# Layer norms brought to features on partitions by 32 by 32 turns on VectorE and two transfers, in place of turns by TensorE

## The chip, the cores and the metric

The kernel runs on one core of a Trainium2 chip. The time is the device time of one launch in microseconds (us). TensorE (PE in the profile) multiplies, VectorE (DVE), ScalarE (ACT) and GpSimd (POOL) do the rest, and SyncE (SP) issues every DMA of this kernel[...].

## What is computed

Four transformer blocks in sequence on x of 16 batches x 256 tokens x 256 features, in float32, 16 heads of 16 features, with a context of 77 tokens per batch and one condition vector per batch. Cut to what matters:

```python
# each of the ten steps below begins with a layer norm of x over the features
def step_norm(x):                         # statistics per token
    h = (x - mean(x)) * rsqrt(var(x) + eps)
    return h * (1 + scale[b]) + shift[b]  # per batch and feature; one step has no modulation

# block 0: self attention with rope and mask (a), attention to the context (ac), MLP (b)
# block 1: attention to the context (cx)
# block 2: self attention (c), attention to the context (cc), MLP (d)
# block 3: self attention with rope (e), attention to the context (ec), MLP (f)
x = x + gate * (softmax(q @ k.T) @ v) @ wo          # attention steps
x = x + gate * (gelu(step_norm(x) @ w1 + b1) @ w2)  # MLP steps, 1024 hidden
```

## The kernel before

x stays in SBUF as x_sb, with tokens on partitions: 128 partitions x (16 batches, 2 halves, 256 features). A matmul contracts over partitions, so a projection of the normed x needs it with features on partitions. `norm_tasks` makes that, once per batch and step, 160 times in all: VectorE takes mean and variance (L467, L468), GpSimd the power -1/2 and the scaled difference xn (L473, L474, L495), TensorE turns xn by four 128x128 transposes through the identity into one PSUM bank (L503), and ScalarE takes the bank into xT with the modulation as scale and bias (L510, or L507 in step cc, which has none). xT is read by the projections (L592 without rope, L644 with rope, L764 for v) or by the first MLP matmul (L1015).

The rest of an attention: scores per head group (L805 self, L817 context), row maxima on VectorE (L831, L835, L839), and these maxima go through DRAM to stand as an extra row beside the queries (L851 turn, L854 store to mrow, L858 load into the tile kq). Then the scores again, transposed and with the maxima in them (L902), exp on ScalarE (L914, L916), the product with v (L925), turns and division (L934, L941, L947, L951), and the output projection with the residual (L972, L978, L985, L988). MLP hidden activations are L1020, the second matmul is L972 too. Gates are loaded by L540 (gb tiles), and L528 adds a bias early.

Nothing is in program order by hand. Every step is a task with an engine, an estimated duration, dependencies and the buffers that it takes or uses (`add`), and a planner (`Order.solve`) runs these through a list schedule. It fixes the order of each engine's instructions, SP's queue among them, before the kernel is built. TensorE takes the ready task with the lowest `prio`, which rises from batch to batch and from step to step; VectorE, ScalarE and GpSimd take what has been ready longest. A transfer has the cost `ISSUE` on SP, 0.45 us, and then a latency `lat`, plus 2.7 us per MB where the task gives a size. [...]

Buffers are counted in `CAPS`: 8 PSUM banks (`b`), one xn, two xT, five kq. A batch is admitted to an attention when a kq tile is free, and holds it until its last L902. The MLP steps wait for all norms of the attention step ahead (`join(norms)`) and, for their matmuls, for its last exponentials. `BY_PE = 2` marks the first two batches of step a, whose mask is added by TensorE.

Of the kernel before, what the change touches and what calls it, by code (L numbers as in the profile page):

```python
# [10 lines left out]
F32 = mybir.dt.float32  # L11
U8 = mybir.dt.uint8
AF = mybir.ActivationFunctionType
# [3 lines left out]
B, N, D, H, HD, LC, FF = 16, 256, 256, 16, 16, 77, 1024  # L17
P = 128
NT = N // P
NC = D // P  # L20
# [53 lines left out]
class Order:  # L74
# [12 lines left out]
    def add(self, eng, dur, run, deps=(), take=(), use=(), prio=0, rp=None, kind=None, joins=(),  # L87
            line=None, last=True, more=0.0, lat=0.0, first=False, mb=0.0):


        t = Task()
        t.joins, t.line, t.last, t.more, t.lat, t.first, t.mb = joins, line, last, more, lat, first, mb
        t.eng, t.dur, t.run, t.prio, t.rp, t.kind = eng, dur, run, prio, rp, kind
        t.deps = [d for d in deps if d is not None]
        t.take, t.held = list(take), list(take) + list(use)
        for h in t.held:
            h.users += 1
        t.outs, t.left, t.ready, t.no, t.since = [], len(t.deps), 0.0, len(self.tasks), None
        for d in t.deps:
            d.outs.append(t)  # L100
        self.tasks.append(t)
        return t
# [111 lines left out]
def pixart_kernel(ctx: ExitStack, tc: tile.TileContext, x, cond_t, ctx_in, mask_c, mask_s, tables, vecs, rows,  # L214
                  mod0, mod1, mod2, mod3, wa, wb, wc, wd, we, wf, out):
    nc = tc.nc
# [4 lines left out]

    CAPS = {"b": 8, "xn": 1, "xT": 2, "kq": 5, "v": 5, "mx": 3, "mr": 2, "ec": 2,
            "ts": 2, "oT": 2, "rope": 2, "qk": 4, "tmp": 2, "gb": 3, "wa": 1, "ctx": 2,
            "cin": 2, "bias": 2, "small": 4, "csmall": 2}

    const = ctx.enter_context(tc.tile_pool(name="const", bufs=1))
    wpool = ctx.enter_context(tc.tile_pool(name="weights", bufs=1))
    work = ctx.enter_context(tc.tile_pool(name="work", bufs=2))
    small = ctx.enter_context(tc.tile_pool(name="small", bufs=4))
    dram = ctx.enter_context(tc.tile_pool(name="dram", bufs=1, space=bass.MemoryType.DRAM))  # L230
# [46 lines left out]
    mrs, vs = [], []  # L277
    for j in range(CAPS["mr"]):
        mrs.append(dram.tile([2, 2, 4, 512], F32, name=f"mrow{j}"))

    for j in range(CAPS["v"]):
        vs.append(const.tile([P, NT, H, 32], F32, name=f"vt{j}"))
# [2 lines left out]
    add = od.add  # L285
    MM = 0.432
    TR = 0.109
    ISSUE = 0.45
    BY_PE = 2
# [40 lines left out]
    t = add("PE", 0.4, rows_turn, take=[h_rt], prio=200)  # L330
    add("DVE", 1.3, late_consts, deps=[t], use=[h_rt], prio=200)
    late_t = od.tasks[-1]
    t = add("ACT", 0.3, silu_exp, prio=200)
# [37 lines left out]
    mods, mod_t = {}, {}  # L371
# [107 lines left out]
    def join(tasks, prio=0):  # L479
        return add("NO", 0.0, lambda: None, deps=tasks, prio=prio)  # L480

    def norm_tasks(s, b, eps, mod, name, prio, deps=()):

        hs, hn, hm, ht = Hold("small"), Hold("xn"), Hold("b"), Hold("xT")

        def stats():
            s["mv"] = norm_stats(x_sb[:, b], P, NT, name)

        def rstd():
            s["rstd"] = rstd_of(s["mv"], P, NT, eps, name)  # L490

        def scale():
            xn = s["xn"] = work.tile([P, NT, D], F32, tag="xn", bufs=CAPS["xn"], name=f"xn_{name}")
            for t in range(NT):
                nc.gpsimd.tensor_scalar(xn[:, t, :], x_sb[:, b, t, :], s["mv"][:, t, 0:1], s["rstd"][:, t:t + 1],  # L495
                                        ALU.subtract, ALU.mult)

        def turn():
            pt = s["pt"] = psum(hm, NC)
            s["xT"] = work.tile([P, NC, N], F32, tag="xT", name=f"xT_{name}")  # L500
            for c in range(NC):
                for t in range(NT):
                    nc.tensor.transpose(pt[:, c, t * P:(t + 1) * P], s["xn"][:, t, c * P:(c + 1) * P], ident)  # L503

        def take():
            if mod is None:
                nc.scalar.copy(s["xT"], s["pt"])  # L507
            else:
                for c in range(NC):
                    nc.scalar.activation(s["xT"][:, c, :], s["pt"][:, c, :], AF.Identity,  # L510
                                         scale=mods[mod][:, 2 + c, b:b + 1], bias=mods[mod][:, c, b:b + 1])
        t1 = add("DVE", 1.0, stats, deps=[x_done[b], *deps], take=[hs], prio=prio)
        t2 = add("POOL", 0.95, rstd, deps=[t1], use=[hs], prio=prio)
        t3 = add("POOL", 2.5, scale, deps=[t2], take=[hn], use=[hs], prio=prio)
        t4 = add("PE", 4 * TR, turn, deps=[t3], take=[hm, ht], use=[hn], prio=prio)
        t5 = add("ACT", 0.6 if mod is None else 1.1, take, deps=[t4, mod_t.get(mod)], use=[hm, ht], prio=prio)
        x_done[b] = t3
        return t5, ht

    def early_add(s, b, pre_add, prio):  # L520

# [164 lines left out]
        a = add("PE", NC * nt * TR, turn, deps=deps, take=[hm], use=[h_dst, *hq], prio=prio)  # L686
        return take(lambda: u["p"], a, [hm, h_dst], prio)

    state = {"mr": 0}

    def attention(b, name, n, wv, wkeys, h_w, w_t, eps, mod, half, biases, masked, pre_add, gate, prio, ctxs=None,
                  barrier=None, after=None, norm_deps=()):

        s, nm = {}, f"{name}{b}"
        self_ = n == N
# [9 lines left out]
        def admit():  # L705
# [5 lines left out]
                  take=[h_kq, h_v], prio=prio,  # L711
                  joins=[("mx", nm), ("mr", nm)] +
                        [(i, (nm, g, kc)) for i in ("e", "av") for g in range(NC) for kc in range(nk)])
        admitted.append(x_t)
        xT_t, hx = norm_tasks(s, b, eps, mod, nm, prio, deps=[x_t])

        norms.append(xT_t)
        if self_:
# [6 lines left out]
        if half is None:  # L725
            hm1, hm2, u = Hold("b"), Hold("b"), {}
# [126 lines left out]
        def move_out():  # L853
            nc.sync.dma_start(s["mr"][0].rearrange("s r (c i j) -> i (s r c) j", i=4, j=32), s["mt"])  # L854

        def move_in():
            for i in range(2):
                nc.sync.dma_start(s["kq"][HD * i:P:32, i], s["mr"][:, i].rearrange("k r n -> r k n"))  # L858
# [491 lines left out]
```

## Time and profile before

| what | value |
|---|---|
| time, median of 3 runs | 2684.58 us (2683.35 to 2687.24) |
| the profiled execution: its time, its span | 2684.49 us, 2682.7 us |
| TensorE busy | 2635.8 us, 98% of the span |
| VectorE, ScalarE, GpSimd busy | 1542.2, 1240.1, 1065.7 us |
| moved by DMA | 60.25 MB |
| granted clock of TensorE, mean | 0.995 |

How to read it: a busy time is the union of the records of an engine; TensorE's matmuls are pipelined, so that the mean duration of one record says less than the distance from group to group. A float32 matmul has two records, a turn one. In a timeline row stand the start, the duration, the engine, the line, the operation, the tile written and the tiles read, the shapes and the count; in brackets stand the engine's idle time ahead of it and what ended it. PEld is the loading of weights into the array.

### The profile page before, as it was taken

The numbers are of one execution on the slowest core, as the hardware profiler recorded it, in microseconds if no ns is written. First come the engines' busy times: TensorE is split into PE (matmuls) and PEld (weight loads), VectorE is DVE, ScalarE is ACT, GpSimd is POOL, SyncE is SP. The second block draws the span as 40 slices with busy tenths as digits, with TensorE's granted clock in tenths as the row PEclk, the third lists the DMA queues.
The fourth block names the chain that finished last, engine by engine and source line by source line (L and its number), as shares of the span: only waits on it lengthen the run. The fifth ranks groups of instructions, "written<-read, shape, count | busy, mean of one in ns | idle before, by whom it ended". The sixth has DMA issues, their size and how long they took to land.

```text
span 2682.7 us, 56475 instructions
## 1 busy us (share of the span) xinstructions
PE 2635.8 (98%) x22144; PEld 1887.2 (70%) x22144; DVE 1542.2 (57%) x4379; ACT 1240.1 (46%) x2495; POOL 1065.7 (40%) x1413
## 2 busy tenths in 40 slices
PE   8999999999999999999999999999999999999999
PEld 5656665766888667666666667888666666667888
DVE  7788886664320566766775664111788876883100
ACT  2444444664332456455555554232455555553332
POOL 4333332545443445133334544433333333562321
PEclk9999999999999999999999999999999999999999
DMA  4000000012110000100000012000000000000000
GB/s 145 14 7 9 10 7 14 16 52 90 31 39 12 25 17 6 35 13 13 20 16 9 5 33 66 16 20 16 11 4 4 4 3 6 5 21 24 20 20 20
DMA packets 53570, 60.25 MB, mean 22 GB/s; under 512 B 19592, under 2 KB 38264, under 8 KB 52536
## 3 DMA queue, kind: packets, MB, share of 16 engines
q1 hardware_dynamic: 53304, 56.65, 7.1%
q8 instruction: 174, 2.85, 0.4%
q14 instruction: 92, 0.75, 0.1%
HBM read 50.44 MB, written 6.19 MB: 21 GB/s over the span
## 4 chain that ended last, share of the span: by engine, by line
PE 92%; DVE 3%; POOL 2%; ACT 1%; issue 1%; DMA 1%; DVEq 0%; ACTq 0%; POOLq 0%; SPq 0%
PE bank L972 20%; PE bank L902 13%; PE bank L1015 12%; PE bank L925 11%; PE bank L805 7%; PE bank L592 7%; PE bank L644 6%; PE bank L764 5%; PE bank L503 3%; PE bank L817 2%; PE bank L684 2%; PE bank L895 2%; PE bank L388 1%; PE bank L579 0%; ACT e_ac L914 0%
## 5 line engine op out<-in xcount | busy, mean ns | idle before, releaser
L902 PE MATMUL bank<-kq 32*128 32x256 f32 (+1 forms) x5120 | 606.2, 396 | 2.9 <-DMA kq<-mrow 2.5
L902 PEld LDWEIGHTS bank<-kq 32*128 32x128 f32 (+1 forms) x5120 | 354.3, 168 | 158.4 <-issue 108.2
L805 PE MATMUL bank<-kq 32*128 32x512 f32 x1536 | 411.1, 638 | 1.9 <-DVE kq L617 1.8
L831 DVE CUSTOM_DVE_ANT_0 junk<-bank,ctxT_masks 128x256 f32<-128x256 f32 x448 | 188.7, 421 | 52.5 <-PE bank L805 21.4
L916 ACT ACTIVATE e_a<-bank 128x512 f32<-128x512 f32 x256 | 137.8, 597 | 175.0 <-PE bank L805 147.1
L916 ACT ACTIVATE e_e<-bank 128x512 f32<-128x512 f32 x256 | 136.1, 599 | 143.9 <-PE bank L805 105.2
L835 DVE TENSOR_REDUCE mx_c<-bank 128x2 f32<-128x512 f32 x256 | 160.2, 681 | 36.8 <-PE bank L805 36.2
L916 ACT ACTIVATE e_c<-bank 128x512 f32<-128x512 f32 x256 | 134.9, 601 | 100.3 <-PE bank L805 74.8
L835 DVE TENSOR_REDUCE mx_e<-bank 128x2 f32<-128x512 f32 x256 | 161.1, 681 | 26.5 <-PE bank L805 25.4
L978 DVE TENSOR_TENSOR x_sb<-x_sb,bank 128x512 f32<-128x512 f32 x80 | 54.8, 685 | 202.3 <-PE bank L972 193.4
L817 PE MATMUL bank<-kq 32*128 32x154 f32 x2048 | 166.9, 309 | 1.3 <-DVE mx_ec L839 0.5
L805 PEld LDWEIGHTS bank<-kq 32*128 32x128 f32 x1536 | 127.4, 184 | 25.2 <-issue 8.1
L817 PEld LDWEIGHTS bank<-kq 32*128 32x128 f32 x2048 | 130.0, 185 | 17.2 <-issue 6.8
L1020 ACT ACTIVATE h_d<-bank,vec 128x256 f32<-128x256 f32 x128 | 53.7, 471 | 156.0 <-PE bank L1015 105.8
L1020 ACT ACTIVATE h_f<-bank,vec 128x256 f32<-128x256 f32 x128 | 53.6, 471 | 153.4 <-PE bank L1015 132.2
L1020 ACT ACTIVATE h_b<-bank,vec 128x256 f32<-128x256 f32 x128 | 53.6, 471 | 146.2 <-PE bank L1015 118.6
L1015 PE MATMUL bank<-xT_b,kq 128*128 128x256 f32 x512 | 113.8, 379 | 0.0
L1015 PE MATMUL bank<-xT_d,kq 128*128 128x256 f32 x512 | 113.6, 380 | 0.0
L1015 PE MATMUL bank<-xT_f,kq 128*128 128x256 f32 x512 | 113.4, 379 | 0.0
L972 PE MATMUL bank<-kq,h_b 128*128 128x256 f32 x512 | 113.2, 379 | 0.0
L972 PE MATMUL bank<-kq,h_d 128*128 128x256 f32 x512 | 113.2, 379 | 0.0
L972 PE MATMUL bank<-kq,h_f 128*128 128x256 f32 x512 | 113.2, 379 | 0.0
(336 smaller groups left out, 5751.4 us busy)
## 6 DMA issues: line engine op xcount, KB each, us to landing
kq<-in_mod_dram SPq DMA_DIRECT2D x10, 512.0 KB
cin<-in_ctx_in_dram SPq DMA_DIRECT2D x36, 128.0 KB
x_sb<-in_x_dram SPq DMA_DIRECT2D x16, 256.0 KB
gb_b<-gate_g0m SPq DMA_DIRECT2D x16, 256.0 KB
gb_c<-gate_g2a SPq DMA_DIRECT2D x16, 256.0 KB
gb_d<-gate_g2m SPq DMA_DIRECT2D x16, 256.0 KB
out_dram<-x_sb SPq DMA_DIRECT2D x16, 256.0 KB
kq<-mrow SPq DMA_DIRECT2D x224, 16.0 KB
```

Source lines behind the costliest of these rows:

```text
L592: nc.tensor.matmul(dst[:, g, :], lhsT=w[:, k, g * P:(g + 1) * P], rhs=xT[:, k, :], start=(k == 0), stop=(k == NC - 1))
L644: nc.tensor.matmul(u["p"][0:r, at:at + D], lhsT=xT()[:, k, t * P:t * P + r], rhs=w()[:, k, :], start=(k == 0), stop=(k == NC - 1))
L805: ls.append(lambda ps=ps, R=R, keys=keys: nc.tensor.matmul(ps.rearrange("p (s k) -> p s k", k=N), lhsT=s["qx"][R, 0, g, t * P:(t + 1) * P] ...
L817: ls.append(lambda ps=ps, R=R, keys=keys, tt=tt: nc.tensor.matmul(ps[:, 2 * tt * n:2 * (tt + 1) * n].rearrange("p (s k) -> p s k", k=n), l ...
L831: nc.vector.tensor_tensor_reduce(junk, u[i][:, i2 * N:(i2 + 1) * N], mb[:, t, :], -1.0, 3.0e38, ALU.add, ALU.min, m[:, i2, g, t:t + 1])
L835: nc.vector.tensor_reduce(m[:, :, g, t], u[i].rearrange("p (s k) -> p s k", k=N), AX.X, ALU.max, negate=True)
L902: (lambda ps=u[i], R=R, q=q: nc.tensor.matmul(ps[0:rows_n, q * N:(q + 1) * N], lhsT=s["kz"][R, q, g, kc * P:kc * P + rows_n], rhs=s["qx"][ ...
L916: nc.scalar.activation(e, u[i][0:rows_n], AF.Exp)
L925: nc.tensor.matmul(u5["p"][32 * r:32 * r + 32, 1 - q, :], lhsT=s["v"][0:rows_n, kc, 8 * g + 2 * r + 1 - q, :], rhs=s["e", g, kc, r][0:rows ...
L972: nc.tensor.matmul(u["p"][:, t, :], lhsT=lhsT(k, t), rhs=w()[:, k, :], start=(k == 0), stop=(k == nk - 1))
L1015: nc.tensor.matmul(u["p"][:, j, :], lhsT=wv["w1"][:, k, f * P:(f + 1) * P], rhs=s["xT"][:, k, :], start=(k == 0), stop=(k == NC - 1))
L1020: nc.scalar.activation(s["h", i][:, j, :], u["p"][:, j, :], func, bias=vcol(b1, 2 * i + j))
```

## The change

Of the 160 norms, 158 no longer go through TensorE; the two of step a with batches 0 and 1 (`direct`) keep the turn by the array. For the others xn is turned by one VectorE instruction in 32 by 32 blocks into y (`turn32`), which reads features with a stride of four, so that later runs are 512 bytes long. y is stored to DRAM (`move_out`, 128 rows of 2 KB), and loaded again with features on partitions into xr (`move_in`, 512 runs of 512 bytes). ScalarE takes xr into xT with the modulation (`take_in`, two instructions). y and xr have one buffer each, the DRAM rows yd two. No PSUM bank is held by these norms. The planner gets the new tasks with their estimates and makes a new order for all engines.

```diff
--- before.py
+++ after.py
@@ -221,7 +221,7 @@
 
     CAPS = {"b": 8, "xn": 1, "xT": 2, "kq": 5, "v": 5, "mx": 3, "mr": 2, "ec": 2,
             "ts": 2, "oT": 2, "rope": 2, "qk": 4, "tmp": 2, "gb": 3, "wa": 1, "ctx": 2,
-            "cin": 2, "bias": 2, "small": 4, "csmall": 2}
+            "y": 1, "yd": 2, "xr": 1, "cin": 2, "bias": 2, "small": 4, "csmall": 2}
 
     const = ctx.enter_context(tc.tile_pool(name="const", bufs=1))
     wpool = ctx.enter_context(tc.tile_pool(name="weights", bufs=1))
@@ -277,6 +277,8 @@
     mrs, vs = [], []
     for j in range(CAPS["mr"]):
         mrs.append(dram.tile([2, 2, 4, 512], F32, name=f"mrow{j}"))
+
+    yds = [dram.tile([P, 512], F32, name=f"yd{j}") for j in range(CAPS["yd"])]
 
     for j in range(CAPS["v"]):
         vs.append(const.tile([P, NT, H, 32], F32, name=f"vt{j}"))
@@ -479,7 +481,7 @@
     def join(tasks, prio=0):
         return add("NO", 0.0, lambda: None, deps=tasks, prio=prio)
 
-    def norm_tasks(s, b, eps, mod, name, prio, deps=()):
+    def norm_tasks(s, b, eps, mod, name, prio, deps=(), direct=False):
 
         hs, hn, hm, ht = Hold("small"), Hold("xn"), Hold("b"), Hold("xT")
 
@@ -512,10 +514,43 @@
         t1 = add("DVE", 1.0, stats, deps=[x_done[b], *deps], take=[hs], prio=prio)
         t2 = add("POOL", 0.95, rstd, deps=[t1], use=[hs], prio=prio)
         t3 = add("POOL", 2.5, scale, deps=[t2], take=[hn], use=[hs], prio=prio)
-        t4 = add("PE", 4 * TR, turn, deps=[t3], take=[hm, ht], use=[hn], prio=prio)
-        t5 = add("ACT", 0.6 if mod is None else 1.1, take, deps=[t4, mod_t.get(mod)], use=[hm, ht], prio=prio)
         x_done[b] = t3
-        return t5, ht
+        if direct:
+            t4 = add("PE", 4 * TR, turn, deps=[t3], take=[hm, ht], use=[hn], prio=prio)
+            return add("ACT", 0.6 if mod is None else 1.1, take, deps=[t4, mod_t.get(mod)], use=[hm, ht], prio=prio), ht
+
+        hy, hd = Hold("y"), Hold("yd")
+
+        def turn32():
+            s["y"] = work.tile([P, 4, NT * NC * 32], F32, tag="y", bufs=CAPS["y"], name=f"y_{name}")
+            nc.vector.transpose(s["y"].rearrange("p f (u i) -> p f u i", i=32),
+                                s["xn"].rearrange("p t (c j f) -> p f (t c) j", j=32, f=4))
+
+        def move_out():
+            s["yd"] = yds[state["yd"] % len(yds)]
+            state["yd"] += 1
+            nc.sync.dma_start(s["yd"], s["y"].rearrange("p f n -> p (f n)"))
+
+        def move_in():
+            s["xr"] = work.tile([P, 4, NT, NC, 32], F32, tag="xr", bufs=CAPS["xr"], name=f"xr_{name}")
+            nc.sync.dma_start(s["xr"].rearrange("p a t c i -> p a (t c i)"),
+                              s["yd"].rearrange("(a j) (f n) -> (j f) a n", j=32, f=4))
+
+        def take_in():
+            s["xT"] = work.tile([P, NC, N], F32, tag="xT", bufs=CAPS["xT"], name=f"xT_{name}")
+            for c in range(NC):
+                to = s["xT"][:, c, :].rearrange("p (t a i) -> p t a i", t=NT, a=4)
+                of = s["xr"][:, :, :, c, :].rearrange("p a t i -> p t a i")
+                if mod is None:
+                    nc.scalar.copy(to, of)
+                else:
+                    nc.scalar.activation(to, of, AF.Identity, scale=mods[mod][:, 2 + c, b:b + 1],
+                                         bias=mods[mod][:, c, b:b + 1])
+        hr = Hold("xr")
+        t = add("DVE", 0.7, turn32, deps=[t3], take=[hy], use=[hn], prio=prio)
+        t = add("SP", ISSUE, move_out, deps=[t], take=[hd], use=[hy], prio=prio, lat=2.0)
+        t = add("SP", ISSUE, move_in, deps=[t], take=[hr], use=[hd], prio=prio, lat=2.0)
+        return add("ACT", 1.1, take_in, deps=[t, mod_t.get(mod)], take=[ht], use=[hr], prio=prio), ht
 
     def early_add(s, b, pre_add, prio):
 
@@ -686,7 +721,7 @@
         a = add("PE", NC * nt * TR, turn, deps=deps, take=[hm], use=[h_dst, *hq], prio=prio)
         return take(lambda: u["p"], a, [hm, h_dst], prio)
 
-    state = {"mr": 0}
+    state = {"mr": 0, "yd": 0}
 
     def attention(b, name, n, wv, wkeys, h_w, w_t, eps, mod, half, biases, masked, pre_add, gate, prio, ctxs=None,
                   barrier=None, after=None, norm_deps=()):
@@ -712,7 +747,7 @@
                   joins=[("mx", nm), ("mr", nm)] +
                         [(i, (nm, g, kc)) for i in ("e", "av") for g in range(NC) for kc in range(nk)])
         admitted.append(x_t)
-        xT_t, hx = norm_tasks(s, b, eps, mod, nm, prio, deps=[x_t])
+        xT_t, hx = norm_tasks(s, b, eps, mod, nm, prio, deps=[x_t], direct=masked and self_ and b < BY_PE)
 
         norms.append(xT_t)
         if self_:
```

## The prediction

> **What bounds the kernel now.** I read the page from the top: engine totals, then the chain that ended last.
>
> ```profile
> span 2682.7 us, 56475 instructions
> PE 2635.8 (98%) x22144; PEld 1887.2 (70%) x22144; DVE 1542.2 (57%) x4379; ACT 1240.1 (46%) x2495; POOL 1065.7 (40%) x1413
> ...
> PE 92%; DVE 3%; POOL 2%; ACT 1%; issue 1%; DMA 1%; DVEq 0%; ACTq 0%; POOLq 0%; SPq 0%
> PE bank L972 20%; PE bank L902 13%; PE bank L1015 12%; PE bank L925 11%; PE bank L805 7%; PE bank L592 7%; PE bank L644 6%; PE bank L764 5%; PE bank L503 3%; PE bank L817 2%; PE bank L684 2%; PE bank L895 2%; PE bank L388 1%; PE bank L579 0%; ACT e_ac L914 0%
> ```
>
> TensorE is idle for only 2682.7 - 2635.8 = 47 us, and 92% of the chain is its work. L503, the turns that the change takes from it, is 3% of the chain. So the turns lie on the path; an idle quarter of another engine would not. Next, the timeline of one MLP block (start, duration, engine, line, tiles, idle before), to see what one turn costs where nothing else disturbs:
>
> ```profile
> 1744.56 7.07 PE L1015 MATMUL bank<-xT_d,kq 128*128 128x256 f32 x32
> ...
> 1751.46 0.60 PE L503 MATMUL bank<-ident,xn_d 128*128 128x128 f32 x4
> ...
> 1751.90 7.07 PE L972 MATMUL bank<-kq,h_d 128*128 128x256 f32 x32
> 1752.17 2.44 POOL L495 TENSOR_SCALAR xn_d<-x_sb,mv_d,rstd_d 128x256 f32<-128x256 f32 x2 [5.38 <-PE bank L503]
> 1752.45 1.02 ACT L510 ACTIVATE xT_d<-bank,mod_2m 128x256 f32<-128x256 f32 x2
> ...
> 1758.81 7.07 PE L1015 MATMUL bank<-xT_d,kq 128*128 128x256 f32 x32
> ```
>
> From one L1015 group to the next is 1758.81 - 1744.56 = 14.25 us, and the two matmul groups alone are 2 x 6.91 = 13.82 us (their durations in the chain in order of time). Four turns cost **0.43 us** of TensorE, not the 4 x 0.273 that their records show, which overlap. Also: POOL waits for TensorE to read the single xn buffer, and xT is ready at 1753.47, 5 us before its matmul.
>
> [...] L858 waits for L854's landing each time (14 waits on mt_cc, 25.2 us). [...] In the trace a change between L902, L925 and full-array matmuls leaves the loader idle for 0.33 to 0.41 us, of which about 0.1 to 0.2 us is lost (the 0.86 us of streaming in L925's group at 614.47 is over at 615.33, the next matmul starts at 615.47).
>
> **Removed.** There are ten stages of 16 norms, 160 in all, of which two keep the array (first stage, batches 0 and 1): 158 x 4 = 632 turns less. At 0.43 us a norm, 158 x 0.43 = **68 us**. In the built order of TensorE, 22 groups of turns stood alone between score matmuls, and changes of mode fall from 1214 to 1175: 39 x 0.15 = 6 us. Sum 74 us. A second reading: 3.0% of 2682.7 is 80.5 us on the chain, x 158/160 = 79.5. I take **74**, and 68 to 80 as ends. One PSUM bank less is held per norm, from turn to take; that can only help, worth 0 to 15 us, and I put none of it into the point.
>
> **Added, engine by engine.** The prices:
>
> ```profile
> L951 DVE STREAM_TRANSPOSE oT_c<-od_c x32: 401/433/446, 1148.6 to 1475.4; 128x256 f32<-128x256 f32 x32
> L934 DVE STREAM_TRANSPOSE ts_c<-bank x32: 674/717/718, 1143.8 to 1469.2; 128x512 f32<-128x512 f32 x32
> ...
> 1426.07 2.28 SPq L858 DMA_DIRECT2D kq<-mrow  x4
> ...
> 1428.45 0.39 SPq L540 DMA_DIRECT2D gb_c<-gate_g2a  x1
> 1431.78 0.53 SPq L854 DMA_DIRECT2D mrow<-mt_cc  x1
> 1431.81 1.28 POOL L528 TENSOR_TENSOR x_sb<-x_sb,gb_c 128x512 f32<-128x512 f32 x1 [3.59 <-DMA gb_c<-gate_g2a]
> ```
>
> - VectorE, one turn32 of 128x512: 0.72 us from L934; at twice that if the stride is paid for. 158 x 0.72 = 114 us (228 at worst), on an engine busy for 1542 of 2683. Cover is thinnest in the first stage: 84.6, 83.1 and 82.3 us busy of each 100 from 100 to 400 us. With a norm per some 21 us it goes to 87% (91% at worst). No bound, but less give. It stands ahead of reductions and of L985's successors in VectorE's queue, and waits there for POOL's L495; that wait is short where the order places it late enough, and TensorE no longer stands between.
> - SP, two issues: 0.4 to 0.7 us each, 316 more, some 160 us on a queue that mostly waits. It costs nothing by itself.
> - Transfers: 256 KB each. L540, as large, lands 1431.81 - 1428.45 = 3.4 us after its issue starts. The store should be like it. The load takes 512 runs of 512 B in place of 128 of 2 KB: 3.4 to 4.5 us. Together about **7 us**, where the planner of the kernel allows 2 x 2.45 = 4.9. So each norm arrives some 2 us later than the order was written for (4 us with a load of 4.5 and a doubled turn; on time if both transfers are as short as L854's 16 KB, which land some 2 us after their issue starts). As to load, 158 x 0.5 MB = 83 MB more over the span is 31 GB/s beside 22; the first 30 us moved up to 373, so bandwidth is no bound.
> - ScalarE: take_in reads SBUF in place of PSUM, two instructions at 0.57 (L510). Only in the stage without modulation is a copy of 0.59 (L507) replaced by two: 16 x 0.55 = 9 us, hidden at 46% busy.
>
> **What of the latency shows.** From xn to xT it was 0.6 + 1.0 us, and becomes 0.7 + 7 + 1.1: some **7 us more** per norm, of which TensorE pays only what finds it out of other work. In MLP stages there is a period of 14 us for one norm, and y, xr and the second xT let the next norms run ahead: nothing. In the self-attention stages there is a period of 21 to 22 us, up to five attentions in flight (kq), and xT lay ready 4.6 us before its use (1962.77 to 1967.37): mostly nothing. In the four cross stages (64 norms, one per 10 us) the lead is 1.6 to 4.2 us (931 to 990 us of the timeline), and a transfer 2 us late eats it: I take 0.15 us on the mean, 10 us. At the three ends of attention ahead of an MLP nothing else is left to run, and the last norm's 7 us come through in part: 3 x 3 = 9 us. TensorE was idle there already: 4.0 us from 600 to 660, 3.6 from 2400 to 2450. At the start of attention behind an MLP (5.2 us idle from 880 to 900) the new buffers let norms be prepared ahead, which gains 2 or 3. The two transfers of batch 2 go in behind the x loads; those end near 30 us, and its matmul came at 44. Given back: 10 + 9 - 3 + 4 for SP's order = **20 us**.
>
> Sum: 2684.5 (the profiled execution, which stands within 0.1 us of the median 2684.58) - 74 + 20 = **2630.5 us**, 2.0% less.
>
> **Rivals.**
> *Cover is complete* (0.10): norms hide everywhere, and the freed bank and buffers fill some of the 47 us: 2684.5 - 80 - 5 = 2600. For it: 98% busy and leads of 4 to 5 us. Against it: the cross stages and the ends.
> *Norms late in every cross stage* (0.22): a load of 4.5 us and a doubled turn make each norm 4 us late against leads of 1.6 to 4.2, so 64 x 0.6 = 38 us, and 16 at the ends: 2684.5 - 74 + 54 = 2664.
> *SP's queue holds up the maxima* (slower, 0.15). [...] In the built order 87 of the 158 loads stand directly behind their store, so SP stands still until it lands, and 53 of 112 stores of row maxima (L854) stand directly behind such a load; in 38 more a norm's transfer lies between L854 and L858. L902 of every attention waits for these. Before, it waited for kq<-mrow only 2.5 us in three waits (6.7 with the loader's), so the lead is unknown. If a late landing costs more than 74/112 = 0.66 us per attention, the gain is gone; at 1 us, with the 10 of the norms, 2684.5 - 74 + 112 + 10 = 2732. Against it: five attentions are in flight and TensorE takes up others' work.
> *It does not do what it says* is excluded: the built order has 8 turns of L503's kind in place of 640, and all other TensorE lines keep their counts.
>
> **Numbers.** The likeliest case (0.53), at 2630, runs from 2612 to 2650. The range goes from 2600 to 2678, to take in the late norms. About 0.2% (5.4 us) is what a measurement here can tell from no change: the cases on the gaining side, less a tail of late norms, give 0.81 faster; 0.04 the same; 0.15 slower.
>
> **What will show it.** L503 with 8 records; MLP periods of 13.8 us; TensorE still near 98% busy, and with some 70 us less of it. turn32 at 0.7 us (or 1.4). A wait of L536 on its store of about 3 us. Where I am wrong: TensorE waits on ACT's xT in the cross stages, or on kq<-mrow, of more than 40 us in sum; or VectorE's L835 and L831 late in the first stage.

## The result, and the profile after

The changed kernel takes **2663.48 us** (median of 4 runs, 2658.88 to 2665.39) against 2685.79 us for the kernel before on the same chip: ratio 0.9916, interval 0.9902 to 0.9931. It is 22 us faster, where the prediction had 54. One of the 84 executions timed for the later experiments, one of e14, fell into a slow state of the chip (3260 us), and e14's median here leaves it out. The page of the kernel after, the lines that answer to those shown of before:

```profile
span 2662.8 us, 55746 instructions
...
PE 2595.9 (97%) x21512; PEld 1821.4 (68%) x21512; DVE 1678.8 (63%) x4537; ACT 1250.2 (47%) x2511; POOL 1062.0 (40%) x1413
...
PE 87%; DVE 6%; POOL 2%; ACT 2%; DMA 1%; issue 1%; DVEq 0%; ACTq 0%; SPq 0%; POOLq 0%
```

TensorE's busy time fell by 2635.8 - 2595.9 = 40 us, not 70, and its idle time rose from 47 to 67 us. In the chain it went from 92% to 87%, and VectorE from 3% to 6%: other engines now end more waits. The timeline of an MLP block shows the removed turn where nothing disturbs it:

```profile
1716.12 7.07 PE L1050 MATMUL bank<-xT_d,kq 128*128 128x256 f32 x32
1723.03 7.07 PE L1007 MATMUL bank<-kq,h_d 128*128 128x256 f32 x32
1729.93 7.07 PE L1050 MATMUL bank<-xT_d,kq 128*128 128x256 f32 x32
```

From one L1050 group to the next it is 1729.93 - 1716.12 = 13.81 us, down from 14.25. So the price of 0.43 us for four turns holds, and a norm there is hidden whole.

To see where the rest went I cut each execution into windows of 4 us and took from them busy time, idle time and granted clock. "Lost to the clock" is the sum over the windows of busy time x (1 - granted clock); "full-clock work" is busy time less that. The last is not work alone: kernels with the very same TensorE instructions differ in it by up to 24 us (no turn at all, e1, and "after, shuffled alike", e14, in this table), so something that goes with the order is in it too. The five kernels below the second row are experiments that follow.

| kernel (profiled execution, us) | span | idle | lost to the clock | full-clock work |
|---|---|---|---|---|
| before | 2682.7 | 46.9 | 11.9 | 2624.0 |
| after | 2662.8 | 66.9 | 19.2 | 2576.7 |
| no turn at all (e1) | 2637.2 | 46.2 | 28.5 | 2562.5 |
| before, shuffled (e12) | 2694.3 | 48.8 | 17.4 | 2628.1 |
| after, shuffled alike (e14) | 2672.4 | 67.2 | 18.8 | 2586.4 |
| no turn, shuffled alike (e18) | 2627.6 | 40.8 | 20.8 | 2566.0 |
| after, copies planned later (e6) | 2648.8 | 53.2 | 21.7 | 2573.9 |

Before to after: 47 us less full-clock work, but 20 us more idle and 7 us more lost to the clock; 47 - 27 = 20, the difference of the spans.

Where the stages lie. An MLP stage begins with its first matmul on xT, cx and e with the first weights that TensorE loads for their first norm or projection, and c with its first product with v (L925, after: L960); interleaved stages are taken together:

| us | a, ac | b | cx | c, cc | d | e, ec | f |
|---|---|---|---|---|---|---|---|
| before | 641.9 | 231.4 | 265.6 | 502.7 | 224.5 | 583.5 | 233.1 |
| after less before | -14.0 | +1.0 | -6.6 | +4.2 | -6.2 | +6.2 | -4.5 |
| e1 less before | -23.6 | -6.3 | +5.1 | -1.2 | -6.1 | -7.2 | -6.2 |
| e6 less before | -7.7 | -4.5 | -7.6 | -3.0 | -4.4 | -2.3 | -4.4 |

At 15 or 16 norms x 0.43 an MLP stage should be 6 to 7 us shorter; two of the three keep most of that. Attention, with 110 of the 158 norms, keeps 14.0 + 6.6 - 4.2 - 6.2 = 10 us of some 110 x 0.43 = 47.

The new rows, first VectorE's turn and the transfers (after: groups of a tile, minimum/median/maximum in ns; then SP's waits: total us, times, longest):

```profile
L526 DVE STREAM_TRANSPOSE y_c<-xn_c x16: 1064/1092/1139, 1050.2 to 1360.3; 128x512 f32<-128x512 f32 x16
```

```profile
SPq L536 <- DMA yd<-y_c: 24.2, 15, 1.7
```

The turn takes 1.09 us, where I had priced 0.72. The transfers are shorter than I had them: a load is issued 2.0 us after its store at the least, 2.3 on the median, and the copy that waits for it starts about 2.9 us later (2313.09 to 2315.92 below). Over the 56 waits for a load that follow, it is 5.3 us (median) from the issue of the store to the start of the copy, in place of 7. What I had not seen coming is a wait of ScalarE. Its waits in the kernel after (total us, times, longest):

```profile
ACT xT_ec L547 <- DMA xr_ec<-yd: 31.2, 10, 5.7
ACT xT_ac L547 <- DMA xr_ac<-yd: 23.7, 11, 3.5
ACT xT_cx L547 <- DMA xr_cx<-yd: 22.0, 9, 8.7
ACT xT_cc L545 <- DMA xr_cc<-yd: 17.8, 9, 3.8
```

All ten stages together give 131 us in 56 waits. One of these waits in the timeline:

```profile
2313.09 0.36 SPq L536 DMA_DIRECT2D xr_ec<-yd  x1
...
2314.09 0.60 PE L719 MATMUL bank<-ident,qr_ec 128*128 128x128 f32 x4
...
2314.61 1.10 PE L937 MATMUL bank<-kq 32*77 32x256 f32 x16
...
2315.92 1.09 ACT L547 ACTIVATE xT_ec<-xr_ec,mod_3x 128x256 f32<-128x256 f32 x2 [4.73 <-DMA xr_ec<-yd]
...
2316.57 2.05 PE L679 MATMUL bank<-w_e,xT_ec 128*128 128x256 f32 x8 [0.85 <-ACT xT_ec L547]
2316.92 1.00 ACT L634 ACTIVATE kq<-bank 128x1024 f32<-128x1024 f32 x1
...
2317.82 2.02 ACT L951 ACTIVATE e_ec<-bank 77x512 f32<-77x512 f32 x4
```

ScalarE stands for 4.73 us before a load that was issued only at 2313.09. Behind it in its queue are L634, whose input (L719) is done at 2314.69, and the exponentials of the scores of L937, done at 2315.71. They run 2.2 and 2.1 us late, with the 1.1 us of L547 itself in that. In the kernel before, ScalarE's waits for the turns of TensorE came to 54 us in 29. The rows of the same four stages:

```profile
ACT xT_ac L510 <- PE bank L503: 9.2, 3, 6.6
ACT xT_cx L510 <- PE bank L503: 8.6, 4, 3.2
ACT xT_cc L507 <- PE bank L503: 6.5, 5, 3.0
ACT xT_ec L510 <- PE bank L503: 3.5, 3, 1.9
```

### The profile page after: what moved, and what is told of

Same layout as the page of the kernel before. It is cut to its first block, busy times and chain, and to the rows that moved or that the text cites. A ratio compares the mean times of both kernels' runs of the same rounds, so it can differ in the third digit from the quotient of the medians.

```text
span 2662.8 us, 55746 instructions
## 1 busy us (share of the span) xinstructions
PE 2595.9 (97%) x21512; PEld 1821.4 (68%) x21512; DVE 1678.8 (63%) x4537; ACT 1250.2 (47%) x2511; POOL 1062.0 (40%) x1413
## 4 chain that ended last, share of the span: by engine, by line
PE 87%; DVE 6%; POOL 2%; ACT 2%; DMA 1%; issue 1%; DVEq 0%; ACTq 0%; SPq 0%; POOLq 0%
PE bank L1007 19%; PE bank L937 13%; PE bank L1050 12%; PE bank L960 11%; PE bank L627 7%; PE bank L840 7%; PE bank L679 6%; PE bank L799 5%; PE bank L852 2%; PE bank L719 2%; PE bank L930 2%; DVE mx_e L870 1%; DVE mx_c L870 0%; DVE mx_ec L874 0%; PE bank L390 0%
## 5 line engine op out<-in xcount | busy, mean ns | idle before, releaser
L937 PE MATMUL bank<-kq 32*128 32x256 f32 (+1 forms) x5120 | 615.8, 397 | 2.3 <-DMA kq<-mrow 0.8
L937 PEld LDWEIGHTS bank<-kq 32*128 32x128 f32 (+1 forms) x5120 | 350.2, 168 | 171.1 <-issue 99.0
L840 PE MATMUL bank<-kq 32*128 32x512 f32 x1536 | 420.5, 642 | 1.9 <-ACT e_e L951 1.6
L852 PEld LDWEIGHTS bank<-kq 32*128 32x128 f32 x2048 | 132.3, 187 | 21.1 <-issue 4.6
L1050 PE MATMUL bank<-xT_b,kq 128*128 128x256 f32 x512 | 117.1, 385 | 0.0
L1050 PE MATMUL bank<-xT_f,kq 128*128 128x256 f32 x512 | 113.5, 379 | 0.0
L1050 PE MATMUL bank<-xT_d,kq 128*128 128x256 f32 x512 | 113.4, 380 | 0.0
L1050 PEld LDWEIGHTS bank<-xT_b,kq 128*128 128x128 f32 x512 | 97.8, 193 | 13.9 <-issue 0.8
```

Source lines behind the costliest of these rows:

```text
L840: ls.append(lambda ps=ps, R=R, keys=keys: nc.tensor.matmul(ps.rearrange("p (s k) -> p s k", k=N), lhsT=s["qx"][R, 0, g, t * P:(t + 1) * P] ...
L852: ls.append(lambda ps=ps, R=R, keys=keys, tt=tt: nc.tensor.matmul(ps[:, 2 * tt * n:2 * (tt + 1) * n].rearrange("p (s k) -> p s k", k=n), l ...
L937: (lambda ps=u[i], R=R, q=q: nc.tensor.matmul(ps[0:rows_n, q * N:(q + 1) * N], lhsT=s["kz"][R, q, g, kc * P:kc * P + rows_n], rhs=s["qx"][ ...
L1050: nc.tensor.matmul(u["p"][:, j, :], lhsT=wv["w1"][:, k, f * P:(f + 1) * P], rhs=s["xT"][:, k, :], start=(k == 0), stop=(k == NC - 1))
```

## The experiments

Times are medians, of four executions in most cases; each ratio is to the kernel before in the same session (2684 to 2688 us), and every diff is against the changed kernel unless it says otherwise.

### The parts of the change: e1 to e3

**e1: no turn, no transfers.** ScalarE copies xn straight into xT.

```diff
-                of = s["xr"][:, :, :, c, :].rearrange("p a t i -> p t a i")
+                of = s["xn"][:, :, c * P:(c + 1) * P].rearrange("p t (a i) -> p t a i", a=4)
...
-        t = add("DVE", 0.7, turn32, ...)
-        t = add("SP", ISSUE, move_out, ...)
-        t = add("SP", ISSUE, move_in, ...)
-        return add("ACT", 1.1, take_in, deps=[t, mod_t.get(mod)], take=[ht], use=[hr], prio=prio), ht
+        return add("ACT", 1.1, take_in, deps=[t3, mod_t.get(mod)], take=[ht], use=[hn], prio=prio), ht
```

> The change with turn32 and both transfers left out: ScalarE takes xT straight from xn, so the 158 norms are not turned at all (that part of the computation is left out). What remains is only that TensorE is rid of 632 turns and their banks. If TensorE's work is what sets the end everywhere (the prediction's sum), 74 us less than before: 2612, and all stages shorter, the self-attention stages c and e by 7 us each. If the self-attention stages are set by something else (banks, VectorE, ScalarE), they keep their length and the whole comes to 2625 to 2645. The difference between this kernel and the changed one (2663) is the price of what was added.

Measured: 2637.09 us, ratio 0.9817 (0.9802 to 0.9831). Removing the turns alone is worth 48 us in time, which lies in the second of the expected ranges: the self-attention stage e is 7 us shorter, c is not. Full-clock work fell by 2624.0 - 2562.5 = 61.5 us; 17 us of that went into more time lost to the clock. The new way costs 2663.5 - 2637.1 = 26 us.

**e2: the turn alone** (take_in reads y), and **e3: the transfers alone** (of xn as it stands).

```diff
# e2
-                of = s["xr"] ...
+                of = s["y"] ...          # no move_out, no move_in
# e3
-            nc.sync.dma_start(s["yd"], s["y"] ...)
+            nc.sync.dma_start(s["yd"], s["xn"] ...)   # no turn32
```

> The change with turn32 kept and both transfers left out: ScalarE takes y (blocks turned, but not moved to their partitions; that part is left out). If VectorE's 1.1 us per norm is what eats the gain, this stays near the changed kernel, 2655 to 2665. If the latency of the transfers eats it, this comes close to the kernel without any turn, within 8 us of it.

> The change with both transfers kept and turn32 left out: xn itself goes out to DRAM and in again (unturned blocks; that part is left out). If VectorE's time is the cause, within 8 us of the kernel without any turn. If the 5 to 6 us of latency, or SP's queue, are the cause, 2655 to 2665, near the changed kernel.

Measured: 2657.10 us (0.9887; 0.9871 to 0.9903) and 2656.31 us (0.9906; 0.9876 to 0.9935), which are 20 and 19 us above e1. The two do not add to 26. They differ in kind: e3 has TensorE idle for 68.1 us (e1: 46.2) and ScalarE waiting 124 us for loads; e2 has 51.8 us idle, no such wait, and 21 us more full-clock work (2583.4), though its TensorE instructions are those of e1. What these 21 us are, is not known.

### Planned durations and the place of ScalarE's copy: e4, e6, e16, e17

**e4: the planner is told the measured prices.**

```diff
-        t = add("DVE", 0.7, turn32, ...)
-        t = add("SP", ISSUE, move_out, ..., lat=2.0)
-        t = add("SP", ISSUE, move_in, ..., lat=2.0)
-        return add("ACT", 1.1, take_in, ...)
+        t = add("DVE", 1.12, turn32, ...)
+        t = add("SP", ISSUE, move_out, ..., lat=1.8)
+        t = add("SP", ISSUE, move_in, ..., lat=2.7)
+        return add("ACT", 1.2, take_in, ...)
```

> The whole change, with the planner's estimates set to what the trace after the change shows: turn32 1.12 us in place of 0.7, the store landing after 2.25 us, the load after 3.15, take_in 1.2. If the gain was lost because the order was made for wrong durations (an engine then waits in its queue for a late norm), 10 us or more are won back: 2640 to 2653. If the durations themselves are what costs, no change within 5 us of 2663, or slower.

Measured: 2669.65 us (0.9940; 0.9925 to 0.9955), 6 us above the changed kernel. ScalarE's wait for loads fell only to 85 us. True prices by themselves bring nothing.

**e6, e16, e17: only the load's latency in the plan** is 4.5, 3.3 and 6.0 us instead of 2.0, which puts L547 later in ScalarE's queue.

```diff
-        t = add("SP", ISSUE, move_in, deps=[t], take=[hr], use=[hd], prio=prio, lat=2.0)
+        t = add("SP", ISSUE, move_in, deps=[t], take=[hr], use=[hd], prio=prio, lat=4.5)
```

> Only the planner's estimate of the load's latency is changed, 2.0 to 4.5 us, so that the copies L545 and L547 stand later in ScalarE's queue, behind exponentials that are ready. Theory 1 (ScalarE stands before a load that has not landed, 112 us in all, and exponentials behind it come late to TensorE): ScalarE's waits for DMA fall to under 40 us, and the time to about 2650 to 2658. Rival (the xT tiles are what TensorE needs next, so that a later copy only delays them): no gain, 2662 to 2675, with TensorE's waits for xT up.

> The estimate of the load's latency in the plan at 3.3 us instead of 2.0 (4.5 gave 2651.0). Theory 1 (ScalarE's standing before a load is a cause of its own): its waits for DMA lie between the 131 us of the changed kernel and the 26 us of the 4.5 case, and so does the time, 2653 to 2661. Rival (the 12.5 us were a lucky order): the time has nothing to do with the waits, and 2665 or more is as likely.

> The estimate at 6.0 us. Theory 1: ScalarE's waits for DMA stay under 26 us and the time is 2646 to 2656, since nothing more is to be won. Rival: 2660 or more.

| latency in the plan, us | 2.0 (after) | 3.3 (e16) | 4.5 (e6) | 6.0 (e17) |
|---|---|---|---|---|
| ScalarE's wait for loads, us | 131 | 68 | 26 | 2 |
| TensorE idle, us | 66.9 | 57.4 | 53.2 | 62.6 |
| time, us | 2663.5 | 2651.5 | 2651.0 | 2662.1 |
| ratio to before | 0.9916 | 0.9877 (0.9844 to 0.9911) | 0.9872 (0.9857 to 0.9887) | 0.9924 (0.9908 to 0.9939) |

ScalarE's waits in e6, for the stages shown above:

```profile
ACT xT_cx L547 <- DMA xr_cx<-yd: 10.9, 2, 8.8
ACT xT_ac L547 <- DMA xr_ac<-yd: 4.5, 2, 2.7
...
ACT xT_ec L547 <- DMA xr_ec<-yd: 4.2, 3, 1.9
ACT xT_cc L545 <- DMA xr_cc<-yd: 0.9, 1, 0.9
```

With it, the rows in which TensorE waits for ScalarE fall from 26.6 us in sum to 9.8 (before: 9.0). But 7.8 us of this fall are one wait at the start of stage cx, which did not go: in e6 TensorE stands there for VectorE's scaling of the context instead.

```profile
PE bank L627 <- DVE ctxT L1229: 8.9, 2, 6.6
```

Without that place the rows for ScalarE fall from 18.8 to 9.8 us, and those for VectorE from 17.0 to 14.5.

The expectation for 4.5 held, and that for 3.3 as to the wait, while the time came out 1.5 us below it. At 6.0 it missed: the wait is gone, but stage a is 13 us longer than in the changed kernel (468.5 against 455.6) and uses up what the other stages gain. TensorE waits for xT only 0.3 us there, so that copies which come too late are not shown to be the reason.

Each of these plans is also another order of all engines, and an order alone moves the time by up to 14 us (e12 to e18 below); e4, with less of the wait, was slower. So one pair says little about the 12 us. Taken together the kernels here that hold the whole change say more. Five have ScalarE waiting for loads for 85 us or more (after, e4, e10, e14, e15): 2663.5 to 2672.4 us, mean 2667. Five have it waiting for 68 us or less (e6, e11, e16, e17, e19): 2648.5 to 2662.1, mean 2654. The two groups do not overlap. So ScalarE's standing before a load is a cause, of about 12 us here and 13 on the mean.

### The length of the turn: e5, e10, e11, e19

**e5: VectorE reads neighbouring words** (the engines' orders are those of the changed kernel). **e10: the same, with GpSimd's scaling writing the features in the order that this needs.** **e11 and e19: e10 with a planned latency of 4.5 and 3.3 us.**

```diff
# e5
-                                s["xn"].rearrange("p t (c j f) -> p f (t c) j", j=32, f=4))
+                                s["xn"].rearrange("p t (c f j) -> p f (t c) j", j=32, f=4))
# e10 has this too, and in scale():
+                if not direct:
+                    to = to.rearrange("p (c f j) -> p c f j", f=4, j=32)
+                    of = of.rearrange("p (c j f) -> p c f j", f=4, j=32)
```

> VectorE's turn reads each 32-column block without the stride of four (the four features of a partition are taken from neighbouring 32-blocks), so the features come out in another order and the output is not the reference's; the planned order of every engine is that of the changed kernel. Theory 1 (the turn is 1.10 us instead of my 0.72 because it reads every fourth word): the row L526 falls to about 0.7 us, 158 x 0.4 = 62 us of VectorE's time, and of the 26 us that are given back some 5 to 10 come back: 2653 to 2658. Rival (the turn's length is hidden, only the order and the two transfers cost): within 3 us of the changed kernel, 2660 to 2666.

> GpSimd's scaling reads and writes in the order that lets VectorE's turn read its 32-column blocks without a stride, so the features come out right; the order of every engine is that of the changed kernel. Theory 1 (the stride costs VectorE 0.4 us a turn, and GpSimd, which is 40% busy, does the reordering for little): L526 about 0.70 us, L497 at most 1.4 us instead of 1.22, the time within 3 us of that of the kernel with the dense turn, 2650 to 2656. Rival (the strided access costs GpSimd more than it saves VectorE): L497 over 1.8 us, and the time 2663 or more.

> The reordering on GpSimd and the load latency of 4.5 us in the plan, together. Theory 1 (the two wins, 10.6 and 12.5 us, have different causes, VectorE's length and ScalarE's standing before a load): about 2642 (2638 to 2647). Rival (both shorten the same wait of ScalarE, so they do not add): 2648 to 2653.

> The reordering on GpSimd, so that VectorE's turn takes 0.70 us, together with 3.3 us for the load's latency in the plan. Theory 1 (the turn's length is worth nothing once the copies stand later): like the kernel with 3.3 us alone, 2646 to 2656. Rival (it adds up): 2638 to 2645.

The rows of e10, whose turn is L530 and whose scaling L501 (after: 1092 and 1224 ns):

```profile
L501 POOL TENSOR_SCALAR xn_c<-x_sb,mv_c,rstd_c x32: 1449/1474/1517, 1045.9 to 1357.7; 128x256 f32<-128x256 f32 x32
L530 DVE STREAM_TRANSPOSE y_c<-xn_c x16: 668/701/711, 1049.4 to 1359.2; 128x512 f32<-128x512 f32 x16
```

Measured: e5 2652.86 us (0.9887; 0.9869 to 0.9906), e10 2664.13 us (0.9921; 0.9901 to 0.9941), e11 2648.54 us (0.9859; 0.9843 to 0.9875), e19 2656.76 us (0.9892; 0.9876 to 0.9909). The stride is the cause of the long turn: 0.70 us without it (e5). e10 fell between its two expectations, and seems to say by what the stride matters: by the norm's latency more than by VectorE's load. In e10 VectorE is freed as in e5 (busy 1625.6 and 1627.7, after 1678.8), but GpSimd's two instructions are 2 x 0.25 = 0.50 us longer while the turn is 0.39 shorter; the way from x to y is about as long as in the changed kernel, and so is the time. (That other work of GpSimd comes later by its longer scaling is not excluded.) In e5 the way is 0.39 us shorter, and 10.6 us are won, 0.07 us a norm, though the order of every engine is the same. e11 is 2.5 us below e6 and e19 is 5.3 us above e16, whose runs spread over 19 us; nothing follows from these two. My 2642 for e11 was a miss: the two gains don't add there. e19 lies just above the 2646 to 2656 of its first theory. e11 is the fastest kernel here with the whole computation, 1.4% below before.

### Which norms: e7 and e8

**e7** keeps TensorE's turns for all attention norms, **e8** for all MLP norms.

```diff
# e7, in the attention task
-        ... direct=masked and self_ and b < BY_PE)
+        ... direct=True)
# e8, in the MLP task
-        xT_t, hx = norm_tasks(s, b, eps, mod, nm, prio, deps=[x_t])
+        xT_t, hx = norm_tasks(s, b, eps, mod, nm, prio, deps=[x_t], direct=True)
```

> Only the MLP's norms take the new way; all norms of the attentions are turned by TensorE as before. Theory 1 (the gain of TensorE's removed turns comes whole where matmuls are dense and no ScalarE work is due, that is in the MLP, 2 stages x 6.2 us, and the attentions win little or nothing net): 2668 to 2675, that is a gain of 10 to 16 us of the 22. Rival (the gain is spread by the number of turns, MLP 32 of 158): a gain of about 5 us, 2680.

> The reverse: the MLP's norms are turned by TensorE, those of the attentions take the new way. Theory 1: what is left of the gain, 22 less 12 = about 8 to 12 us, so 2674 to 2678, though 126 of the 158 turns are taken off TensorE. Rival (by the number of turns): 0.8 x 22 = 18 us, 2667.

(The 32 MLP norms in these expectations should read 48, three stages of 16, and the 126 of the attentions 110; by the number of turns the rival is then 7 us for e7 and 15 for e8.)

Measured: e7 2685.70 us (1.0004; 0.9993 to 1.0014), e8 2666.52 us (0.9934; 0.9913 to 0.9956). Theory 1 fell: it expected a gain of 10 to 16 us for e7, and for e8 at least 7 us more time than measured. Yet the MLP stages do what it says. b, d and f are 4.8, 6.2 and 6.2 us shorter, and full-clock work falls by 2624.0 - 2602.7 = 21.3 us, which is 48 x 0.44. In the profiled execution, one of the slowest of e7's twelve (2690.14 us), all of it comes back elsewhere: 33.0 us are lost to the clock instead of 11.9 (+21.1), and 5.7 us are added to the idle time, in attention stages whose instructions are the same and only stand in another order. The clock is no fixed price of an order either: from 2679.1 to 2690.2 us e7's mean granted clock goes from 0.991 to 0.987, and 0.004 of 2685 is those 11 us. e8 loses less to the clock than before (9.8, in its fastest execution). That led to the next question.

### Is an order worth something by itself? e12 to e15 and e18

One number of the plan that has nothing to do with the change is set a little wrong; the work stays, and the order of every engine is shuffled. e12 and e13 are against the kernel before, e14 and e15 against the changed kernel, e18 against e1 (like e1, it has neither turn nor transfers).

```diff
# e12, e14, e18
-        t3 = add("POOL", 2.5, scale, deps=[t2], take=[hn], use=[hs], prio=prio)
+        t3 = add("POOL", 2.6, scale, deps=[t2], take=[hn], use=[hs], prio=prio)
# e13, e15
-        t1 = add("DVE", 1.0, stats, deps=[x_done[b], *deps], take=[hs], prio=prio)
+        t1 = add("DVE", 1.1, stats, deps=[x_done[b], *deps], take=[hs], prio=prio)
```

> The kernel before, unchanged in its work; the planner is told 2.6 instead of 2.5 us for GpSimd's scaling, which only shuffles its order. Theory 1 (a plan's order alone moves the time by the number of short half-clock stretches it happens to cause, and the order of before was a lucky one with 13.6 us lost): 2688 to 2705, with 20 to 35 us lost to the clock. Rival (the order is worth nothing by itself; the clock loss of the changed kernel belongs to the change): 2681 to 2688, with 10 to 18 us lost.

> As the last, with 1.1 instead of 1.0 us for the statistics on VectorE. Theory 1: 2688 to 2705. Rival: 2681 to 2688.

> The changed kernel, its work the same, with the planner told 2.6 instead of 2.5 us for GpSimd's scaling: only the order is shuffled. Theory 1 (any shuffle costs before 10 to 15 us, so before had a lucky order and the changed kernel an ordinary one): within 6 us of the changed kernel, 2657 to 2670. Rival (both kernels sit on orders that a shuffle makes worse, so the difference between them holds for ordinary orders too): 2672 to 2682.

> As the last, with 1.1 instead of 1.0 us for the statistics on VectorE. Theory 1: 2657 to 2670. Rival: 2672 to 2682.

> The turn on VectorE and the two transfers left out (so the output is not the reference's), now with the shuffle that cost 11 us in before and 10 in the changed kernel. Theory 1 (the removed turns are worth some 48 us at an equal order, and only 26 us are given back by the new way): 2637 plus about 10, 2643 to 2652. Rival (2637 was no lucky order and the removed turns are worth more): 2634 to 2641.

| order | before | no turn | after | gain of removing | cost of the new way | net |
|---|---|---|---|---|---|---|
| as planned | 2685.3 | 2637.1 | 2663.5 | 48.2 | 26.4 | 21.8 |
| scaling 2.6 | 2696.15 (1.0049; 1.0034 to 1.0064) | 2629.19 (0.9789; 0.9768 to 0.9810) | 2672.41 (0.9958; 0.9945 to 0.9971) | 67.0 | 43.2 | 23.7 |
| statistics 1.1 | 2699.68 (1.0053; 1.0038 to 1.0068) | not run | 2667.02 (0.9940; 0.9922 to 0.9959) | | | 32.7 |

A shuffle moves the time of a kernel by -8 to +14 us with no change of its work. The kernel before stands on an order 11 and 14 us better than its two shuffles, the changed kernel 9 and 4. e12, e13 and e15 came out as theory 1 has it as to the time, e14 just as its rival has it. So neither holds alone: over three orders the luck of before's order explains some 4 us of the missing gain (mean net 26.1 against 21.8), at one of them 11, and a net gain of 22 to 33 us stands at all three. For the clock, e12's and e13's expectations count the loss over whole windows, idle time too: 13.6 us before, 18.8 in both, under the 20 expected. The clock is about half of the price of e12's order: of its 11.6 us, nearly all in stage a, 5.5 are lost to the clock, 1.9 are idle time, and 4.1 stand as full-clock work, though TensorE's instructions are the same. e18 was a miss in the other direction: its order is better than that of e1.

## Why the prediction was wrong

**The sum, "- 74 + 20".** The sign and the range (2600 to 2678) held, the point did not. At the kernel's own order the two terms measure -48 and +26, so that of the 32 us which the forecast missed, 26 lie in the first and 6 in the second; at the second order they measure -67 and +43, and it is 7 and 23. The net is nearly the same; how it divides depends on the order.

**The first term, 74, was mis-sized, mostly not in its price.** 0.43 us a norm is right where it was read (14.25 to 13.81 in MLP). Over all norms full-clock work falls by 61.5 us (e1) and 62.1 (e12 to e18), which is 0.39 a norm; but e2, with e1's TensorE instructions, has it fall by 40.6, so this is no sure figure, and whether the 6 us for changes of mode came cannot be told. The step that failed is the one from TensorE's work to time: I took it that the time falls by all that is taken from TensorE. It does not: between before and e1, 17 of the 61.5 us went into the clock, and at the other order the time gained 5 us more than the full-clock work. Why e1's order loses 28.5 us to the clock and e18's 20.8 stays open. The second reading, 80, from L503's share of the chain, was further off. The bank that comes free, 0 to 15 us of gain, was not tested by itself.

**The second term, 20, was too small, and it had the wrong carrier.** I let a late norm cost TensorE only where it waits for xT itself, and wrote of ScalarE "hidden at 46% busy". Two of my prices erred in opposite directions: the turn 1.09 us in place of 0.72, the transfers 5.3 in place of 7. Together, 6.4 us, they are below the 7.7 that I had. What failed is the question of who is queued behind the waiting instruction. I asked it for SP and for VectorE; I did not ask it for ScalarE, and there it costs about 12 us. The direct waits for xT are small but for one, which the next paragraph is about:

```profile
PE bank L627 <- ACT xT_cx L547: 7.8, 1, 7.8
PE bank L679 <- ACT xT_ec L547: 0.9, 1, 0.9
PE bank L937 <- DMA kq<-mrow: 0.8, 1, 0.8
```

The indirect ones are not. Less the waits for xT, the rows of TensorE's waits for ScalarE sum to 17.9 us (before 6.9), those for VectorE to 17.0 (before 11.1); e6 brings the first back to 9.8, and 12.5 us of time with it. The remaining 14 us of the cost at this order, and the 43 at the other, I could not divide between VectorE's turn and the two transfers, since e2 and e3 each cost some 20 us and their orders differ.

**"-3" at the start of attention behind an MLP** had the wrong sign. There stands the one long wait for xT, 7.8 us, and after it TensorE works at half speed (the same eight matmuls take 3.78 us, ahead of it 1.89); the stretch from b to cx's first product with v goes from 42.0 to 47.9 us. It is not the transfers' doing alone: e1, without them, takes 47.7. Nor would an earlier xT have saved the 7.8 us: the context that cx needs next is scaled by VectorE until 885.1 us, and in e6, which turns to the context first, TensorE waits there for 8.9 us; the stretch takes 44.3.

```profile
883.39 1.68 DVE L1229 TENSOR_TENSOR ctxT<-ctxT,mod_1k 128x1232 f32<-128x1232 f32 x1
```

**The rivals.** "Norms late in every cross stage", 2664, whose doubled turn and load of 4.5 us were estimates of mine that no trace of before shows, meets the time within a microsecond, but not by its mechanism: of the four cross stages, each from its first product with v on, ac, cx and cc are 4.5, 12.5 and 3.4 us shorter than before, only ec is 7.1 longer, and apart from the start of cx TensorE stands before xT for 0.9 us there. "SP's queue holds up the maxima" fell: TensorE waits 0.8 us for kq<-mrow (before 2.5), and SP issues a store of row maxima 0.07 us (mean) after the maxima are turned, as before. "Cover complete" is nearest to MLP stages alone.

**What was to show it.** L503's successor has 8 records; the MLP period is 13.8 us; L536 waits on its store, with a longest wait of 1.7 us for c and 3.4 at most, where I said about 3. TensorE has 40 us less of busy time, not 70, and is 97% busy. The first stage, where I feared for VectorE's cover, is 9.5 us shorter.

## What to carry to other kernels

When an operand moves from a producer with a sure time to a transfer, ask who is queued behind the instruction that takes it in, on its own engine, even if that engine is half idle. Place that instruction later in its queue by trial, on both sides: here 3.3 or 4.5 us in the plan is 12 us better than 2.0, and 6.0 is not; the measured durations by themselves (e4) were no help. And where a planner orders everything, shuffle the order of both kernels before believing a difference of some ten microseconds.

## What the runs showed of the hardware

**TensorE's granted clock fell to half, once with no idle time ahead of it.** The long wait above looks as if it had brought the clock down. In the timeline of the kernel after, the same eight matmuls before and after it:

```profile
870.83 1.89 PE L627 MATMUL bank<-xT_cx,w_c 128*128 128x256 f32 x8
...
883.40 3.78 PE L627 MATMUL bank<-xT_cx,w_c 128*128 128x256 f32 x8 [7.79 <-ACT xT_cx L547]
```

But the clock had fallen before the wait began. Windows of the kernel after: the window and its length, busy time of TensorE, its loader, VectorE, ScalarE and GpSimd (with instructions), TensorE's granted clock, DMA share, GB/s:

```profile
872.00:876.00 4.00, 2.93 (x20) 2.40 (x18) 0.79 (x4) 1.26 (x2) 3.81 (x5) 0.87 0.17 61
876.00:880.00 4.00, 0.00 (x0) 0.00 (x0) 3.19 (x8) 0.00 (x0) 2.66 (x3) 0.50 0.17 66
```

The wait begins at 883.40 - 7.79 = 875.61 us. A mean of 0.87 over four us is 1.04 us at half clock, so the clock was down from about 875.0, ahead of the wait, which did not start the fall; whether it kept the clock down is not shown. In the kernels before and after the clock falls twelve times within the span, and in the 4 us ahead of each fall TensorE was idle for 3.09 us at the most (before, at 895.57 us) and not at all at the least (before, at 946.77 us). e12 too shows half clock with hardly any idle time. Windows of e12:

```profile
384.00:388.00 4.00, 4.00 (x56) 2.21 (x60) 2.60 (x14) 3.14 (x5) 0.00 (x0) 1.00 0.11 33
388.00:392.00 4.00, 3.66 (x50) 2.57 (x44) 3.82 (x13) 0.05 (x1) 0.00 (x0) 0.89 0.00 0
392.00:396.00 4.00, 4.00 (x26) 1.72 (x22) 0.94 (x4) 1.35 (x3) 0.00 (x0) 0.50 0.01 4
396.00:400.00 4.00, 4.00 (x32) 1.84 (x28) 1.33 (x8) 1.91 (x4) 0.00 (x0) 0.50 0.00 0
```

Only 0.34 us are idle, and the clock is halved for at least the next 8 us. What precedes it, from 387.73 to 390.71 us, are the matmuls of L817 on 32 rows and of L812 on one row of the array; whether that has to do with the fall, no run here tests. It matters to the case: TensorE loses 9.8 to 33.0 us to the clock in the kernels here, more or less by order and by execution, and a table of waits shows none of it.

**A stride of four words cost this 32 by 32 turn 57%.** The prediction allowed up to double for it, an estimate of mine that no trace of before shows; measured are 1.10 us with it and 0.70 without (e5), on 128x512 float32. The same stride in GpSimd's scaling costs 0.25 us on 1.22 (e10).
